# Attention block and octonion feed-forward on one core: score banks shared between heads, masked maxima in two plain operations, two transfers per placed maximum, weight loads on ScalarE's queue, idle products at the start

## The chip, the cores and the metric

The kernel runs on one NeuronCore of one Trainium2 chip. The core has five engines with a queue each: TensorE (PE; its weight loads are listed apart as PEld), VectorE (DVE), ScalarE (ACT), GpSimd (POOL) and SyncE (SP), which here only issues DMA transfers. The metric is the device time of one execution in microseconds. It was measured in five runs, and their median is compared.

## What is computed

The input x is 2 x 1024 x 512, float32. It is normalised per row, and the normalised rows go two ways: through causal attention with 32 heads of 16 and a position bias (ALiBi), and through a feed-forward layer whose weights are octonion-structured and reduced to three values. The result is x + attention x silu(feed-forward).

```
xn = layernorm(x)
qkv = xn @ w_qkv.T + b_qkv ; q, k, v: 32 heads of 16
scores = q k^T / sqrt(16) + slope[h] * (key - 1023), -1e9 above the diagonal
s = softmax(scores) v, then @ w_out.T + b_out
Wq = mean|W| * clip(round(W / mean|W|), -1, 1)      for w_gate, w_up, w_down
M[k, i] = sign(k, i) * Wq[j(k, i)]                  64 blocks from 8
g = silu(M_down (silu(M_gate xn) * (M_up xn)))
out = x + s * g
```

## The kernel before

**Stages.** A lead-in normalises the first batch's eight row blocks (`normal`, lines 205 to 219), transposes them into `xnT` (`norm_item`) and makes the first q, k and v. The attention stage follows, and with it all that can be done beside it: the other q, k and v products (`qk_items`, `v_items`), reducing the weights to signs (`ternary_sum`, `ternary_total`, `ternary_signs`), turning the down weights, normalising the second batch, and the output products. The feed-forward tail (lines 1193 to 1345) comes last and runs gate, up and down over four blocks of 512 rows.

**Units of attention.** A unit is a batch b, a group g of four heads and a half qc of the queries (512 of 1024): 32 units. Each has two passes over its scores. The first pass (`max_items`) finds the row maximum: queries on partitions, a product per tile tl of 128 queries and head i, in a PSUM bank of its own from the two banks of `ps_x`. For qc = 1 the 512 keys to the left are reduced by a plain `tensor_reduce` (line 507). The block up to the diagonal, (tl + 1) x 128 keys wide, goes through one fused operation that adds a mask over the full width, writes the sum to a scratch tile and leaves the maximum in an accumulator, starting from the left maximum (line 510; the profile lists the accumulator's read as an instruction of its own). `split_max` splits the maxima into a high and a low part; `place_max` turns them with four PE transposes, ACT copies them to `mr`, and four DMA transfers issued by POOL, one per head, put them into two extra rows of the unit's q stack (line 551).

The second pass (`exp_step`) has keys on partitions: a product per key tile kt of 128 keys and head (line 571) in a bank of the three of `ps_e`; with the extra rows the product is the score minus its maximum. In the key tiles on the diagonal only the queries from the diagonal on are computed, so widths are 512, 384, 256 and 128, each in its own bank, and a bf16 product of an identity with a triangular mask is added to the first 128 columns (`mask_step`, line 582). ACT takes the exponential of the bank (`exp_of`, line 586) into a tile `p` of four heads. `value_step` multiplies p with v for the four heads in four column strips of PE (line 599) and adds up over the key tiles in one bank; `normalise` divides.

**Order.** The order of PE's queue is written by a planner in the kernel itself (from line 704): it keeps modelled clocks of PE (`now`), ACT and DVE, the times at which banks come free (`e_free`, `x_free`, `m_free`) and a cost for each item, and emits the next item by readiness and priority (`next_max`, `next_exp`, `next_turn`, `next_value`, `next_side`, `next_behind`, `step`). A maximum's placing is taken to have landed 3.5 us after ACT's copy. Matmuls are pinned in program order by `pe`. Instructions that are not pinned may be moved ahead on their engine by the framework's scheduler; in the profile, loads of x and the loads of `bo_sb` and `wo_sb` are issued far ahead of their place in the program.

**Queues.** POOL issues the weight loads (`load_weight`: one transfer and two for a swapped copy), all but the first of the q/k weights (`load_wq`, two transfers each), and the placings. SP issues x, the spills of q and k (`st` to `sp`), the refills of the q and k stacks (`fill_q`, `fill_k`) and the outputs. The weight tiles share the two slots of `vp` with v, so w_u is loaded when the signs of w_g have been stored (`keep_signs`), and w_d when those of w_u have. On POOL, `v_items` fills the v tile with ones (line 379) when its first product is emitted; before that, at line 874, stand the compacting of the second q/k weights (line 131) and the fills of two k stacks.

Of the kernel before, what the change touches and what calls it, by code (L numbers as in the profile page):

```python
# [19 lines left out]
P = 128  # L20
# [39 lines left out]
def kernel(  # L60
# [21 lines left out]

    NP = NG // 2
# [23 lines left out]
    nc.gpsimd.memset(ones, 1.0)  # L107
# [10 lines left out]
    def load_wq(gp, eng):  # L118
        t = wqp.tile([P, 2, KD, 2, 4, 32], F32, tag="wqr", name=f"wqr_{gp[0]}_{gp[1]}")
        for n in range(2):  # L120
            eng.dma_start(
                out=t[:, n].rearrange("p k w h e -> p (k w h e)"), in_=wqk[2 * gp[1] + n]
            )
        wq_raw[gp] = t
# [51 lines left out]
    def load_x(t, eng):  # L176
# [3 lines left out]
        eng.dma_start(out=xt, in_=x[t * P : (t + 1) * P, :])  # L180
# [42 lines left out]
    mask16 = aw.tile([P, P], BF16, name="mask16")  # L223

    def make_mask():
# [5 lines left out]
            pattern=[[1, P]],  # L231
# [5 lines left out]

    def pe(ins):

        return tc.keep_in_program_order(ins)  # L240
# [22 lines left out]
    def load_weight(src, name):  # L263
        w = vp.tile([P, 8, H8], F32, tag="v", name=f"w_{name}")
        nc.gpsimd.dma_start(out=w[0:64].rearrange("p j o -> p (j o)"), in_=src)
        pairs = src.rearrange("p (j s o) -> p j s o", s=2, o=H8)
        swapped = w[64:128].rearrange("p (j s) o -> p j s o", s=2)
        for n in range(2):
            nc.gpsimd.dma_start(out=swapped[:, :, n, :], in_=pairs[:, :, 1 - n, :])
# [100 lines left out]

    def v_items(b, hh):
# [3 lines left out]
        def product(kt, c):  # L375
            if kt == 0 and c == 0:
                v = vp.tile([P, 8, 16 * VC + 16], F32, tag="v", name=f"v_{b}_{hh}")
                v_tiles[b, hh] = v
                nc.gpsimd.memset(v, 1.0)
# [30 lines left out]
    def qk_items(b, gp):  # L410
# [3 lines left out]
        def product(which, c, kt):  # L414
# [20 lines left out]
            if (which, c, kt) == (1, n > 1, KD - 1) and n < B * NP:  # L435
                load_wq((n // NP, n % NP), nc.gpsimd)
# [48 lines left out]
    def max_items(b, g, qc):  # L485
# [3 lines left out]
        def step(tl, i, c):  # L489
            if (tl, i, c) == (0, 0, 0):  # L490
                tiles["mx"] = wk.tile([P, 4, 4], F32, tag="mx", name=f"mx_{b}_{g}_{qc}")
                tiles["part"] = wk.tile([P, 16], F32, tag="part", name=f"mp_{b}_{g}_{qc}")
            t = 4 * qc + tl
            n = 512 if c < qc else (tl + 1) * P
            ps = ps_x.tile([P, 512], F32, tag="x", name=f"s1_{b}_{g}_{t}_{c}_{i}")
            pe(
                nc.tensor.matmul(  # L497
                    ps[:, :n],
                    lhsT=q_of(b, g, qc)[0 : NR - 2, i, tl * P : (tl + 1) * P],
                    rhs=k_of(b, g, c)[0 : NR - 2, i, :n],  # L500
                    start=True,
                    stop=True,
                )
            )
            pm = tiles["part"][:, tl * 4 + i : tl * 4 + i + 1]
            if c < qc:
                nc.vector.tensor_reduce(pm, ps, AX.X, ALU.max)  # L507
                return
            scr = wk.tile([P, 512], F32, tag="scr", name=f"scr_{b}_{g}_{t}_{i}", bufs=1)
            nc.vector.tensor_tensor_reduce(  # L510
                out=scr[:, :n],
                in0=ps[:, :n],
                in1=mask[:, 512 - n : 512],
                scale=1.0,
                scalar=pm if qc else -3.0e38,
                op0=ALU.add,
                op1=ALU.max,
                accum_out=tiles["mx"][:, tl, i : i + 1],
            )

        return [
            (512 if c < qc else (tl + 1) * P, lambda tl=tl, i=i, c=c: step(tl, i, c))
            for tl in range(4)
            for c in range(qc + 1)
            for i in range(4)
        ], tiles

    def split_max(b, g, qc, tiles):

        mx = tiles["mx"]  # L530
        rm = wk.tile([P, 4, 4, 2], F32, tag="rm", name=f"rm_{b}_{g}_{qc}")
        tiles["rm"] = rm
        nc.vector.tensor_copy(rm[:, :, :, 0].bitcast(F32R), mx)
# [884 lines left out]
```

## Time and profile before

| | us |
|---|---|
| median of 5 runs | 1187.65 |
| fastest and slowest run | 1187.31, 1193.19 |
| the profiled execution | 1193.19 |
| its span, first to last instruction | 1191.4 |
| lead-in, until the first score product | 0 to 53.2 |
| attention stage, last exp product of a unit | to 897.1 |
| feed-forward tail, end | 1191.4 |

The mean granted clock of TensorE is 0.972. The costliest groups of the page, with busy time and mean duration, then the idle time of the engine just before them and what ended it:

```profile
L586 ACT ACTIVATE p<-s 128x512 f32<-128x512 f32 (+3 forms) x768 | 324.0, 495 | 294.0 <-PE s L582 189.8
L497 PE MATMUL s<-k_stack,q_stack 126*128 126x512 f32 (+3 forms) x768 | 307.0, 441 | 9.9 <-DVE mx L510 4.9
L571 PE MATMUL s<-q_stack,k_stack 128*128 128x512 f32 (+3 forms) x768 | 253.7, 394 | 31.7 <-DMA q_stack<-mr 21.7
...
L507 DVE TENSOR_REDUCE mp<-s 128x1 f32<-128x512 f32 x256 | 169.1, 686 | 73.8 <-PE s L497 72.4
...
L510 DVE CUSTOM_DVE_ANT_0 scr<-s,mask,mp 128x128 f32<-128x128 f32 (+3 forms) x256 | 140.3, 548 | 82.8 <-PE s L497 67.7
L510 DVE CUSTOM_DVE_ANT_0 scr<-s,mask 128x128 f32<-128x128 f32 (+3 forms) x256 | 125.0, 488 | 100.6 <-PE s L497 82.7
...
L582 PE MATMUL s<-mask,ident 128*128 128x128 bf16 x512 | 68.5, 226 | 0.0
```

A line reads: line of the kernel, engine, operation, result and operands, shapes, count; then busy microseconds and the mean nanoseconds of one; then idle time before. A mean over several shapes ("+3 forms") is no duration of any of them. Durations of matmuls overlap, so the step from one start to the next tells more than the duration.

### The profile page before, as it was taken

The page shows a single profiled execution, that of the slowest core. Times are in us where ns is not written, and L with a number is a line of the kernel's source. Part 1 is how long each engine was busy: PE and PEld are TensorE (multiplying, and loading weights), DVE is VectorE, ACT ScalarE, POOL GpSimd, SP SyncE. Part 2 cuts the span into 40 slices and gives each one's busy share as a digit, 9 for nine tenths or more (in the row PEclk, how much of TensorE's full clock was granted, in tenths as well). Part 3 has the DMA queues.
Part 4 walks back from the last instruction along what each step waited for, and adds up shares of the span by engine and source line. Part 5 has one row for each costly group of instructions (what it writes and reads, how often), then busy time and mean ns, then how long its engine had stood idle before and what let it go on. Part 6 is the DMA issues. An engine that isn't in the chain of part 4 may idle for free.

```text
span 1191.4 us, 16717 instructions
## 1 busy us (share of the span) xinstructions
PE 1089.8 (91%) x5714; PEld 688.5 (58%) x5714; DVE 604.4 (51%) x1714; ACT 526.7 (44%) x1166; POOL 220.9 (19%) x381
## 2 busy tenths in 40 slices
PE   4899589898999799998999999999989999999997
PEld 2544355555645565554555655555445677878775
DVE  5267543666746576565665645667743113131211
ACT  5024475446644346544464444455675213222222
POOL 8311250011110200021100010101100113232322
PEclk9899889999999899999999999999999999999999
DMA  7994445335431743543633515542014112111120
GB/s 251 189 191 147 107 117 108 60 82 99 80 57 48 136 70 56 124 99 75 123 59 53 85 52 122 116 81 50 23 47 152 36 53 73 34 54 54 33 73 35
DMA packets 74964, 104.31 MB, mean 88 GB/s; under 512 B 29040, under 2 KB 32208, under 8 KB 74880
## 3 DMA queue, kind: packets, MB, share of 16 engines
q1 hardware_dynamic: 66336, 87.48, 33.0%
q0 software_dynamic: 8256, 14.72, 5.1%
q8 instruction: 45, 0.74, 0.3%
q10 hardware_dynamic: 288, 1.05, 0.2%
q14 instruction: 39, 0.32, 0.1%
HBM read 69.58 MB, written 33.10 MB: 86 GB/s over the span
## 4 chain that ended last, share of the span: by engine, by line
PE 32%; issue 14%; DMA 2%; ACT 2%; POOL 2%; DVE 2%; DVEq 0%; POOLq 0%; ACTq 0%
PE pg L1253 6%; PE pu L1253 6%; PE pd L1287 5%; PE s L571 4%; PE po L599 3%; PE s L497 3%; PE pout L668 3%; DMA q_stack<-mr 1%; POOL q_stack L551 1%; ACT p L586 1%; DMA out_dram<-y 1%; DVE scr L510 1%; PE s L582 1%; POOL hs L1270 1%; POOL y L1304 0%
## 5 line engine op out<-in xcount | busy, mean ns | idle before, releaser
L586 ACT ACTIVATE p<-s 128x512 f32<-128x512 f32 (+3 forms) x768 | 324.0, 495 | 294.0 <-PE s L582 189.8
L497 PE MATMUL s<-k_stack,q_stack 126*128 126x512 f32 (+3 forms) x768 | 307.0, 441 | 9.9 <-DVE mx L510 4.9
L571 PE MATMUL s<-q_stack,k_stack 128*128 128x512 f32 (+3 forms) x768 | 253.7, 394 | 31.7 <-DMA q_stack<-mr 21.7
L497 PEld LDWEIGHTS s<-k_stack,q_stack 126*128 126x128 f32 x768 | 141.4, 194 | 126.4 <-DVE mx L510 52.4
L507 DVE TENSOR_REDUCE mp<-s 128x1 f32<-128x512 f32 x256 | 169.1, 686 | 73.8 <-PE s L497 72.4
L571 PEld LDWEIGHTS s<-q_stack,k_stack 128*128 128x128 f32 x768 | 143.8, 195 | 98.7 <-ACT p L586 37.5
L510 DVE CUSTOM_DVE_ANT_0 scr<-s,mask,mp 128x128 f32<-128x128 f32 (+3 forms) x256 | 140.3, 548 | 82.8 <-PE s L497 67.7
L510 DVE CUSTOM_DVE_ANT_0 scr<-s,mask 128x128 f32<-128x128 f32 (+3 forms) x256 | 125.0, 488 | 100.6 <-PE s L497 82.7
L551 POOL DMA_DIRECT2D q_stack<-mr x128 | 63.9, 504 | 581.1 <-ACT mr L549 516.9
L599 PE MATMUL po<-p,v 128*32 128x512 f32 (+3 forms) x1536 | 148.9, 497 | 0.0
L426 PE MATMUL pqk<-xnT,wq 128*128 128x512 f32 x256 | 132.2, 616 | 2.5 <-ACT xnT L353 1.4
L1264 DVE SCALAR_TENSOR_TENSOR h<-pu,sc_u,sg 128x512 f32<-128x512 f32 (+1 forms) x44 | 33.1, 751 | 166.4 <-PE pu L1253 160.1
L1270 POOL TENSOR_TENSOR hs<-h,hs 128x512 fp32r<-128x512 f32 (+1 forms) x44 | 57.7, 1311 | 185.5 <-ACT hs L1269 185.5
L599 PEld LDWEIGHTS po<-p,v 128*32 128x32 f32 x1536 | 42.3, 109 | 65.7 <-issue 54.3
L384 PE MATMUL pv<-wv,xnT 128*128 128x256 f32 x256 | 74.4, 409 | 5.5 <-DVE v L395 4.7
L1262 ACT ACTIVATE sg<-pg,sc_g 128x512 f32<-128x512 f32 (+1 forms) x44 | 30.2, 687 | 100.7 <-PE pg L1253 95.7
L582 PE MATMUL s<-mask,ident 128*128 128x128 bf16 x512 | 68.5, 226 | 0.0
L668 PE MATMUL pout<-wo_sb,oT 128*128 128x512 f32 x128 | 62.5, 603 | 0.9 <-ACT oT L659 0.5
L1269 ACT CAST hs<-h 128x512 fp32r<-128x512 f32 (+1 forms) x44 | 27.3, 620 | 75.0 <-DVE h L1264 75.0
L426 PEld LDWEIGHTS pqk<-xnT,wq 128*128 128x128 f32 x256 | 45.1, 194 | 23.9 <-issue 17.1
L441 ACT ACTIVATE st<-pqk,bqk_sb 128x512 fp32r<-128x512 f32 x32 | 22.1, 691 | 78.2 <-PE pqk L426 45.1
L384 PEld LDWEIGHTS pv<-wv,xnT 128*128 128x128 f32 x256 | 48.1, 204 | 14.8 <-DVE v L395 5.1
(157 smaller groups left out, 1130.9 us busy)
## 6 DMA issues: line engine op xcount, KB each, us to landing
sp<-st SPq DMA_DIRECT2D x32, 512.0 KB
q_stack<-sp SPq DMA_DIRECT2D x128, 128.0 KB
k_stack<-sp SPq DMA_DIRECT2D x128, 128.0 KB
wqr<-in_wqk_dram POOLq DMA_DIRECT2D x14, 512.0 KB, 7.2
xt<-in_x_dram SPq DMA_DIRECT2D x16, 256.0 KB
att<-o SPq DMA_DIRECT2D x32, 128.0 KB
ot<-att SPq DMA_DIRECT2D x16, 256.0 KB
proj<-y SPq DMA_DIRECT2D x16, 256.0 KB
```

What stands on the lines that cost most here:

```text
L384: nc.tensor.matmul(ps[:, 0:256], lhsT=xnT[:, c, b * S + kt * P : b * S + (kt + 1) * P], rhs=wv_tiles[2 * b + hh][:, c, :], start=(c == 0), ...
L426: nc.tensor.matmul(ps, lhsT=wq_tiles[b, gp][:, kt, which, :], rhs=xnT[:, kt, b * S + c * 512 : b * S + (c + 1) * 512], start=(kt == 0), st ...
L497: nc.tensor.matmul(ps[:, :n], lhsT=q_of(b, g, qc)[0 : NR - 2, i, tl * P : (tl + 1) * P], rhs=k_of(b, g, c)[0 : NR - 2, i, :n], start=True, ...
L507: nc.vector.tensor_reduce(pm, ps, AX.X, ALU.max)
L510: nc.vector.tensor_tensor_reduce(out=scr[:, :n], in0=ps[:, :n], in1=mask[:, 512 - n : 512], scale=1.0, scalar=pm if qc else -3.0e38, op0=A ...
L551: nc.gpsimd.dma_start(out=q[NR - 2 : NR, i, :].bitcast(F32), in_=mr[2 * i : 2 * i + 2, :].bitcast(F32),)
L571: nc.tensor.matmul(ps[:, :w], lhsT=k[0:NR, i, kt % 4 * P : (kt % 4 + 1) * P], rhs=q[0:NR, i, 512 - w : 512], start=True, stop=(kt < 4 * qc),)
L582: pe(nc.tensor.matmul(ps[:, 0:P], lhsT=ident16, rhs=mask16, start=False, stop=True))
L586: nc.scalar.activation(p_tiles[b, g, qc, kt][:, i, :w], ps[:, :w], AF.Exp, scale=0.25)
L599: nc.tensor.matmul(po[32 * i : 32 * i + 32, 512 - w : 512], lhsT=v[:, kt, h * VC : h * VC + 32], rhs=pr[:, i, :w], start=(kt == 0), stop=( ...
L668: nc.tensor.matmul(ps, lhsT=turned[t][:, c, :], rhs=wo_sb[:, c, :], start=(c == 0), stop=(c == KD - 1),)
L1253: nc.tensor.matmul(ps[:fs, :], lhsT=fw[mt][:, n0 + kt, 0:fs], rhs=part[:, kt, :], start=(kt == 0 and n == 0), stop=(kt == KD - 1 and n == 1),)
```

## The change

It has seven parts.

1. In the first pass the diagonal blocks of several heads share a bank: four heads at 128 keys, two at 256, one at 384 and 512. Their maximum is taken by an addition of the mask in place, on the 128 x 128 diagonal blocks alone, and a plain reduction over the whole bank, one result per head. The left maxima have a tile of their own and are joined in `split_max`.
2. In the second pass the diagonal key tiles are put into cells of full banks: 512; 384 and 128 of the same head; 256 of two heads. One mask product covers both blocks of a bank.
3. The parts of the maxima are laid out by part, and placing takes two transfers of four rows in place of four of two rows.
4. `load_weight` for w_u and w_d and the later `load_wq` are issued by ACT; w_g stays with POOL.
5. The loads of x, of q/k weights, of the three weights, and of `bo_sb` and `wo_sb` are pinned in program order on their queue.
6. `begin_v` fills the v tile with ones; the first is called ahead of the compacting of the second q/k weights.
7. Twenty products of a tile of ones stand first on PE; the ones are set by DVE instead of POOL.

The planner's costs are changed with them: a maximum costs DVE 1.04 per column plus 70, and 135 per head plus 70 for the mask; every exp costs ACT 510; a mask product 55 per block.

```diff
-    nc.gpsimd.memset(ones, 1.0)
+    nc.vector.memset(ones, 1.0)
...
-        eng.dma_start(out=xt, in_=x[t * P : (t + 1) * P, :])
+        pe(eng.dma_start(out=xt, in_=x[t * P : (t + 1) * P, :]))
...
-    mask16 = aw.tile([P, P], BF16, name="mask16")
+    mask16 = aw.tile([P, 2, P], BF16, name="mask16")
...
-    def load_weight(src, name):
+    def load_weight(src, name, eng):
         w = vp.tile([P, 8, H8], F32, tag="v", name=f"w_{name}")
-        nc.gpsimd.dma_start(out=w[0:64].rearrange("p j o -> p (j o)"), in_=src)
+        pe(eng.dma_start(out=w[0:64].rearrange("p j o -> p (j o)"), in_=src))
...
+    def begin_v(b, hh):
+        v_tiles[b, hh] = vp.tile([P, 8, 16 * VC + 16], F32, tag="v", name=f"v_{b}_{hh}")
+        nc.gpsimd.memset(v_tiles[b, hh], 1.0)
...
-                load_wq((n // NP, n % NP), nc.gpsimd)
+                load_wq((n // NP, n % NP), nc.scalar)
...
+        def left(tl, i):
+            if (tl, i) == (0, 0):
+                begin()
+            ps = products(tl, i, 1, 0, 512)
+            nc.vector.tensor_reduce(tiles["left"][:, tl, i : i + 1], ps, AX.X, ALU.max)
+
+        def diagonal(tl, first, count):
+            if (qc, tl, first) == (0, 0, 0):
+                begin()
+            n = (tl + 1) * P
+            ps = products(tl, first, count, qc, n)
+            block = ps[:, :, tl * P : n]
+            nc.vector.tensor_tensor(
+                block,
+                block,
+                mask[:, 384:512].rearrange("p (h n) -> p h n", h=1).to_broadcast([P, count, P]),
+                ALU.add,
+            )
+            nc.vector.tensor_reduce(
+                tiles["mx"][:, tl, first : first + count], ps, AX.X, ALU.max
+            )
...
+            count = (4, 2, 1, 1)[tl]
...
         mx = tiles["mx"]
-        rm = wk.tile([P, 4, 4, 2], F32, tag="rm", name=f"rm_{b}_{g}_{qc}")
+        if qc:
+            nc.vector.tensor_tensor(mx, mx, tiles["left"], ALU.max)
+        rm = wk.tile([P, 4, 2, 4], F32, tag="rm", name=f"rm_{b}_{g}_{qc}")
...
-        for i in range(4):
+        for n in range(2):
             nc.gpsimd.dma_start(
-                out=q[NR - 2 : NR, i, :].bitcast(F32),
-                in_=mr[2 * i : 2 * i + 2, :].bitcast(F32),
+                out=q[NR - 2 + n : NR - 1 + n].bitcast(F32),
+                in_=mr[4 * n : 4 * n + 4, :].bitcast(F32),
             )
...
+    def cells_of(qc):
+        d = 4 * qc
+        return [((kt, 0, 512),) for kt in range(d)] + [
+            ((d, 0, 512),),
+            ((d + 1, 0, 384), (d + 3, 384, 128)),
+            ((d + 2, 0, 256),),
+        ]
...
+        for kt, h, c0, w in pieces:
+            pe(
+                nc.tensor.matmul(
+                    ps[:, c0 : c0 + w],
+                    lhsT=k_of(b, g, kt // 4)[0:NR, h, kt % 4 * P : (kt % 4 + 1) * P],
+                    rhs=q[0:NR, h, 512 - w : 512],
+                    start=(c0 == 0),
+                    stop=(kt < 4 * qc),
+                )
+            )
...
+        if len(pieces) == 1:
+            out, rhs = ps[:, 0:P], mask16[:, 0, :]
+        else:
+            step = pieces[1][2]
+            out = ps.rearrange("p (c n) -> p c n", n=P)[:, 0 :: step // P, :]
+            rhs = mask16
+        pe(nc.tensor.matmul(out, lhsT=ident16, rhs=rhs, start=False, stop=True))
...
+        nc.scalar.activation(p[:, c : c + 512], ps, AF.Exp, scale=0.25)
...
-            lambda: load_weight(w, name),
+            lambda: load_weight(w, name, nc.scalar),
...
+    idle = ps_e.tile([P, 512], F32, tag="e", name="idle")
+    for n in range(20):
+        pe(nc.tensor.matmul(idle[:, 0:P], lhsT=ones, rhs=ones, start=True, stop=True))
...
-    quick(lambda: (compact_wq((0, 1)), add_ring(early, 2, 2)))
+    quick(lambda: (begin_v(0, 0), compact_wq((0, 1)), add_ring(early, 2, 2)))
...
-    later(lambda: nc.gpsimd.dma_start(out=bo_sb, in_=bo.partition_broadcast(P)))
+    later(lambda: pe(nc.gpsimd.dma_start(out=bo_sb, in_=bo.partition_broadcast(P))))
...
-            run_pe("R", ready, max(cost * 0.417 + 18, 108))
-            full = cost == 512 and units[u][2] == 1 and n // 4 % 2 == 0
-            end = run_dve(now[0] + 150, 600 if full else cost * 1.0 + 220)
+            run_pe("R", ready, heads_in * max(cost * 0.417 + 18, 108))
+            end = run_dve(
+                now[0] + 150,
+                heads_in * cost * 1.04 + 70 + (heads_in * 135 + 70) * diagonal,
+            )
```

## The prediction, made before the changed kernel was run

> **What bounds it now.** The page's busy row comes first, then the granted clock by slice, then windows, then the waits of PE, then the timeline where a wait is long.
>
> ```profile
> PE 1089.8 (91%) x5714; PEld 688.5 (58%) x5714; DVE 604.4 (51%) x1714; ACT 526.7 (44%) x1166; POOL 220.9 (19%) x381
> ...
> PEclk9899889999999899999999999999999999999999
> ```
>
> PE is busy nine tenths of the span, and below full clock in early slices. The windows view puts the attention stage, which the change edits, apart from the feed-forward tail, which it leaves alone (286 us):
>
> ```profile
> 45.00:905.00 860.00, 792.18 (x4498) 464.99 (x4498) 519.99 (x1591) 434.57 (x1014) 109.72 (x218) 0.96 0.44 92
> 905.00:1191.00 286.00, 271.99 (x1136) 209.26 (x1136) 64.76 (x75) 74.27 (x119) 78.57 (x59) 0.99 0.16 53
> ```
>
> A busy PE is not a full one. Between 45 and 905 us I took the step from each matmul record's start to the next and subtracted its streaming time: 616 us of 859 is streaming. Some 31 us more are excess at half clock (61 us of half-clock windows); the other 211 us are steps lengthened by waits and by going from one kind of product to another. So the order of PE's queue and the waits in it set the end. PE's matmul waits, then its weight-load waits (which run partly under a matmul, so they bound from above):
>
> ```profile
> PE s L571 <- DMA q_stack<-mr: 21.7, 13, 6.1
> ...
> PE tot_d L281 <- DVE wsum_d L275: 9.5, 1, 9.5
> PE s L571 <- ACT p L586: 9.1, 13, 1.9
> PE s L497 <- DVE mx L510: 4.9, 12, 2.2
> PE pv L384 <- DVE v L395: 4.7, 1, 4.7
> ```
>
> ```profile
> PEld s L497 <- DVE mx L510: 52.4, 168, 2.5
> ...
> PEld s L571 <- ACT p L586: 37.5, 110, 2.3
> ...
> PEld s L497 <- DVE mp L507: 27.1, 82, 1.9
> ```
>
> The reader sees three kinds: a placed maximum that lands late, two long stalls early on, and hundreds of short waits for a score bank.
>
> **The change, part by part.** The sum is made against the profiled execution: 1193.2 us, a span of 1191.4 and 1.8 around it. It is the slowest of five runs, 5.5 above the median of 1187.65; I take the sum off the median.
>
> *Ones filled ahead (begin_v).*
>
> ```profile
> 38.37 1.95 POOL L131 COPY wq<-wqr 128x128 f32<-128x128 f32 x8 [9.90 <-issue]
> ...
> 40.39 3.55 POOL L149 MEMSET k_stack<- 64x2048 f32 x2
> ...
> 44.00 2.02 POOL L379 MEMSET v<- 128x2304 f32 x1
> ...
> 46.53 6.99 PE L384 MATMUL pv<-wv,xnT 128*128 128x256 f32 x18 [4.73 <-DVE v L395]
> ```
>
> POOL idles 9.9 us until PE has read the old wq, then copies, fills two k stacks and only then v. Filled first, v is ready near 31 us and the 4.7 us stall goes. The clock is at half from 45.5 to 52.3 us, behind that stall: 3.4 us more. Next late would be the q rows of the first maxima: their transfer landed at 41.3 us, before the value products end, so nothing new stalls. I take -7, ends -8 and -3.
>
> *Idle products.* Twenty f32 products are 40 records (L281 shows two a product). At 109 to 220 ns (later and first transposes of 128 columns) they last 4.4 to 8.8 us, under PE's wait for the first row block until 12.7. They may warm the clock: the first 16 records of pqk take 8.59 us, the second 16 take 7.13. I take -1; ends -2.3, and +1 if the ones come behind both k fills on DVE.
>
> *Weights on ScalarE's queue.* The down weights before:
>
> ```profile
> 126.14 1.09 POOL L121 DMA_DIRECT2D wqr<-in_wqk_dram  x2 [0.30 <-POOL wq L131]
> ...
> 137.34 0.63 POOL L269 DMA_DIRECT2D w_d<-in_wd_dram  x1 [5.46 <-DMA wqr<-in_wqk_dram]
> ...
> 142.66 0.58 PE L281 MATMUL tot_d<-wsum_d,ones 64*128 64x1 f32 x2 [9.54 <-DVE wsum_d L275]
> ```
>
> The third transfer stood behind wqr's. Without it: the store of w_u's signs landed at 128.5, three issues take 1.8 us, landing 7.4 to 8.6 (w_u's), the sum 1.6: near 140, a stall of 6.6 instead of 9.5, so -3. But the transfer waits for that store, now in ACT's own queue: ACT may stand from 124.2 to 130, with the exps behind it, and PE behind them once three banks are full. Ends -16 (stall and its 13.7 us of half clock gone) and +6. For w_u ACT stands about 73 to 80; its first exp came at 80.6, so 0, worst +3. Seven wq loads put 14 issues of 0.40 us on ACT (5.6 us, under PE where it waits for nothing of ACT), and each may wait for older transfers: the trace has SyncE take 6.15 us for four q fills at 394 us. I take 1 us a load, +7, ends 0 and +45. Pinned x loads come later: blocks 8 and 9 were normalised before the first exp, 10 and 11 together; now up to three more table pairs of 2 x 1.28 us on ACT, +2, ends 0 and +8. The pinned bo and wo loads leave 47 to 67 us; nothing waits for them: 0. Part: +6.
>
> A page speaks against this part. The Trainium skill, "DMA: Bandwidth & Descriptors", section "Issuing engines are not separate DMA queues", says that all transfers share the same engines and another issuing engine saves only sequencer time. The 5.46 us wait above disagrees for this queue; by the page the -3 and the -4 of the next part would be 0.
>
> *Two transfers per placing.*
>
> ```profile
> L551 POOL DMA_DIRECT2D q_stack<-mr x128 | 63.9, 504 | 581.1 <-ACT mr L549 516.9 <-ACT p L586 34.0 <-issue 30.1
> ```
>
> Four issues take 2.0 us, two take 1.0, so the last row lands up to 1 us earlier. Of 13 waits with 21.7 us, 0.6 to 1 us each goes: -8. The longest, 6.1 us at 401.6, stood behind wqr's 1 MB on POOL's queue (landing 7.8 us, 1.4 when quiet): -4. Half-clock windows follow several (216, 298, 342, 400, 544, 643 us: 24 us, 12 lost): -4. Part -16, ends -33 and -6.
>
> *Shared banks.* Score banks fall from 768 + 768 to 608 + 576: a unit's diagonal maxima take 11 banks for 16, its diagonal exps 10 for 16; products and columns stay. The three weight-load waits are 117.0 us over 1536 banks; 23% fewer banks, -27. By the matmul waits of the same rows (17.2 us), -4. Nearer to the first, as steps from score to score are long where no idle is shown: -15.
>
> *DVE's own work.* Steps from start to start when busy: fused add-and-maximum 209, 340, 482, 616 ns for 128 to 512 columns (first half; 276 to 676 in the second), its accumulator read 226. A diagonal costs 10.2 or 11.2 us. After: adds with their durations plus 33 ns, since a reduce reads them (as at a dependent pair of L626 and L627): 724 + 2x454 + 8x318; reduces 7x602 + 4x470; 10.3 us. Level, so 0; it lies beside PE. Over 32 units DVE's ends are -11 us (second halves cost 0.9 less each, first halves nothing) and, with every row's duration counted whole (285, 421, 691 for adds, 686 and 553 for reduces), 10.8 us a diagonal against 9.1 and 10.1, +39; they cost the end only where the cover is gone, which the bank term's far end and the first rival hold.
>
> Here too a page differs: "VectorE: DVE Perf Modes", section "The DRAIN you can't avoid", holds that the next op starts only when the pipe is empty. The trace has reduces of 686 ns start 598 to 607 ns apart, so they overlap. By the page the whole-duration end would hold, and the bank term would be near 0.
>
> *Masks.* 512 records become 320, columns alike. They come in 224 runs of 2.3; at that length 85 runs go. Entering and leaving one costs 57 and 100 ns over streaming: -13. The weight loads' waits there (12.5 us) give -5. I take -9, ends -14 and -3. ACT: four exps of 477, 371, 264, 157 ns make 5.1 us a unit; ten of 477 make 4.8; off the path, 0. The one extra maximum for second halves (0.2 us on DVE, 16 times) has an end of +3: 0.
>
> Sum: -7 -1 +6 -16 -15 -9 = **-42 us**, 1187.65 - 42 = **1146 us**. Ends all at once would be -100 and +50; they aren't one cause.
>
> **Rivals.** *DVE paces the scores.* If maxima set the beat, fewer banks bring nothing: DVE does 10.3 us a diagonal either way, and a PE that waits less for placing waits for DVE. Against it: DVE sits idle 222.8 us for score products. Then -7 -1 +6 -8 -3 = -13: 1175.
>
> *ACT stands behind its own loads.* Nine places (seven wq, w_u, w_d) where transfers wait in the queue that runs the exps. For: SyncE's issues do take up to 6 us for four; the store took 4.3 us to land. Against: PE waits for ACT in 37.5 us of weight loads alone, and qk products stand beside the loads. The other parts give -48; from 5.3 us of PE per place it is lost. At 45 + 6 + 3 + 8 = 62: +14, 1202, slower.
>
> *The order eats it.* Costs in the hand-written order change, so the whole queue is laid anew; new waits may replace old ones: 1187, within 0.3%.
>
> **How the numbers follow.** Chances: forecast 0.59 (its own range 1112 to 1168), DVE 0.20, ACT 0.16, no change 0.05. A measurement tells about 0.3% (3.6 us) from nothing. Faster 0.79, same 0.05, slower 0.16. The range 1110 to 1192 leaves out the slow case and the far fast end.
>
> **What would show it.** Right: v's memset before the copies and no stall at 46 us; 64 placing transfers, their waits under 10 us; 320 masks; the three bank waits below 100 us; an attention stage near 820 us with the tail still 286. Wrong: ACT waiting on transfers for more than 20 us, PE's score waits on ACT grown, tot_d still late, or bank waits above 117 us.

## The result and the profile after

The changed kernel takes 1190.65 us (median of 38 runs, 1184.12 to 1196.33), the kernel before 1187.63 us (64 runs). The ratio is 1.003, interval 1.0019 to 1.0042: slower by about 3.6 us, where 42 less were forecast. Below, every difference is such a ratio to runs of the kernel before on the same chip, times 1187.6 us; the two profiled executions (1193.19 and 1186.91 us) lie on opposite sides of their medians, so their spans are not compared.

The page's busy row and clock row of the changed kernel, then two windows, the attention stage and the tail (columns: window, length, busy time and instructions of PE, PEld, DVE, ACT, POOL, then granted clock, DMA share, GB/s):

```profile
PE 1075.2 (91%) x5562; PEld 684.4 (58%) x5562; DVE 662.5 (56%) x1411; ACT 506.6 (43%) x972; POOL 176.9 (15%) x296
...
PEclk9998988999899999999999998999999999999998
```

```profile
45.00:895.00 850.00, 766.13 (x4292) 450.48 (x4291) 578.50 (x1291) 414.03 (x814) 66.16 (x135) 0.96 0.44 93
895.00:1185.00 290.00, 271.42 (x1139) 208.41 (x1137) 65.20 (x75) 76.62 (x129) 78.61 (x59) 0.98 0.16 55
```

From the first score product to the last value product it is still 843.5 us (845.0 before); it was to be some 25 us less. (The execution before lies 5.6 us above its median and this one 3.7 below, so by the medians the stage is no shorter at all.) PE has less to do there than before (766 us busy for 792), and so has ACT, but VectorE is busy 58 us longer (578.5 for 520.0). The lead-in did get shorter: the first score product starts at 45.8 us instead of 53.2. PE's matmul waits and weight-load waits now (in total, times, longest):

```profile
PE s L501 <- DVE mx L529: 19.9, 47, 1.5
PE pt L673 <- DVE st L446: 18.0, 2, 16.0
PE s L617 <- DMA q_stack<-mr: 7.0, 3, 3.8
...
PE s L617 <- ACT p L639: 5.3, 4, 3.0
...
PE s L501 <- DVE left L515: 2.8, 9, 0.8
...
PE tot_d L283 <- DVE wsum_d L277: 2.0, 1, 2.0
```

```profile
PEld s L617 <- ACT p L639: 28.9, 86, 3.3
...
PEld s L501 <- PE s L617: 20.8, 43, 0.9
PEld s L501 <- DVE left L515: 19.8, 59, 1.4
...
PEld s L501 <- PE s L501: 17.5, 40, 1.0
...
PEld s L501 <- DVE mx L529: 3.2, 8, 0.8
```

Most waits of the table before shrank: placing from 21.7 to 7.0, w_d's sum from 9.5 to 2.0, the exps' from 37.5 to 28.9. Two took their place. PE's score products stand 19.9 us for the maxima of the diagonal, where it was 4.9; and one stall of 16.0 us is new.

The weight loads' wait for those maxima seems to have gone (52.4 before, 3.2 now), but that is a matter of names. The two rows that end in `PE s` are not in the profile before. With a third of 2.5 us they make 40.8 us in 90 waits, and 36.7 of these end within 0.2 us after a reduce of L529, so they are waits for the maxima too. With them the prediction's three bank waits are 88.6 us for 117.0: they fell by 28.4 us, where it had reckoned 27 for 23% fewer banks. PE's own waits on the same three rows, in which no product runs, rose from 17.2 to 28.0. The groups that make the maxima, busy time and mean, then idle time before:

```profile
L515 DVE TENSOR_REDUCE left<-s 128x1 f32<-128x512 f32 x256 | 170.0, 686 | 94.5 <-PE s L501 93.0
L529 DVE TENSOR_REDUCE mx<-s 128x1 f32<-128x384 f32 (+3 forms) x352 | 217.8, 636 | 4.8
...
L523 DVE TENSOR_TENSOR s<-s,mask 128x128 f32<-128x128 f32 (+2 forms) x352 | 120.6, 355 | 96.4 <-PE s L501 92.1
```

217.8 + 120.6 us of plain operations stand where the fused operation took 140.3 + 125.0 and its accumulator reads 42.4.

The new stall, in the timeline (start, duration, instructions, idle before and what ended it; SPq and ACTq are the queues that issue transfers):

```profile
62.58 22.40 SPq L484 DMA_DIRECT2D q_stack<-sp  x4
...
80.69 0.82 ACTq L126 DMA_DIRECT2D wqr<-in_wqk_dram  x2
...
85.50 0.51 SPq L299 DMA_DIRECT2D signs_dram<-w_g  x1
86.75 1.97 SPq L449 DMA_DIRECT2D sp<-st  x2
...
89.24 0.54 ACTq L267 DMA_DIRECT2D w_u<-in_wu_dram  x1
...
93.49 0.69 ACT L445 ACTIVATE st<-pqk,bqk_sb 128x512 fp32r<-128x512 f32 x1 [12.35 <-DMA sp<-st]
95.66 1.56 DVE L277 TENSOR_REDUCE wsum_u<-w_u 64x1 f32<-64x1360 f32 x1 [13.35 <-DMA w_u<-in_wu_dram]
...
97.94 0.90 PE L673 MATMUL pt<-ident,posb 128*128 128x128 f32 x3 [16.04 <-DVE st L446]
```

It is to be read from the top. SyncE needs 22.4 us for four refills of a q stack; the signs of w_g, behind them in its queue, leave at 85.5 us instead of 72.6; w_u can only then be loaded. Behind the signs stand two spills of q and k, so ACT has a free `st` only at 93.5 us. VectorE, which fills the other half of `st`, first stands for w_u, and PE for VectorE. What held SyncE is in the waits of its own queue:

```profile
SPq L471 <- DMA wqr<-in_wqk_dram: 53.9, 4, 30.0
...
SPq L697 <- DMA wqr<-in_wqk_dram: 28.8, 1, 28.8
...
SPq L484 <- DMA wqr<-in_wqk_dram: 20.2, 1, 20.2
```

SyncE's transfers wait 103.8 us in seven places for loads of q/k weights with which they share no data; before, when POOL issued those, it was 1.4 us. Each load now stands in ACT's queue behind the exps, and SyncE's transfers behind the load: the longest wait begins at 561.5 us, and ACT issues the load at 587.8.

### The profile page after: what moved, and what is told of

Same layout as the page of the kernel before. It is cut to its first block, busy times and chain, and to the rows that moved or that the text cites. A ratio compares the mean times of both kernels' runs of the same rounds, so it can differ in the third digit from the quotient of the medians.

```text
span 1185.1 us, 15629 instructions
## 1 busy us (share of the span) xinstructions
PE 1075.2 (91%) x5562; PEld 684.4 (58%) x5562; DVE 662.5 (56%) x1411; ACT 506.6 (43%) x972; POOL 176.9 (15%) x296
## 4 chain that ended last, share of the span: by engine, by line
PE 71%; DVE 11%; DMA 7%; issue 5%; ACT 3%; POOL 2%; SPq 0%; ACTq 0%; DVEq 0%; POOLq 0%
PE s L501 12%; PE s L617 11%; PE po L653 10%; PE pqk L430 8%; PE pg L1322 6%; PE pu L1322 6%; PE pd L1356 5%; PE pout L722 4%; PE pv L388 3%; DVE mx L529 3%; DVE s L523 2%; PE s L634 2%; DMA q_stack<-mr 1%; DVE left L515 1%; PE pm L566 1%
## 5 line engine op out<-in xcount | busy, mean ns | idle before, releaser
L639 ACT ACTIVATE p<-s 128x512 f32<-128x512 f32 x576 | 303.0, 598 | 214.6 <-PE s L634 133.8
L501 PE MATMUL s<-k_stack,q_stack 126*128 126x512 f32 (+3 forms) x768 | 282.5, 431 | 26.5 <-DVE mx L529 19.9
L617 PE MATMUL s<-q_stack,k_stack 128*128 128x512 f32 (+3 forms) x768 | 223.7, 376 | 13.3 <-DMA q_stack<-mr 7.0
L515 DVE TENSOR_REDUCE left<-s 128x1 f32<-128x512 f32 x256 | 170.0, 686 | 94.5 <-PE s L501 93.0
L529 DVE TENSOR_REDUCE mx<-s 128x1 f32<-128x384 f32 (+3 forms) x352 | 217.8, 636 | 4.8
L501 PEld LDWEIGHTS s<-k_stack,q_stack 126*128 126x128 f32 x768 | 135.9, 197 | 123.5 <-issue 34.3
L617 PEld LDWEIGHTS s<-q_stack,k_stack 128*128 128x128 f32 x768 | 137.4, 195 | 70.4 <-ACT p L639 28.9
L523 DVE TENSOR_TENSOR s<-s,mask 128x128 f32<-128x128 f32 (+2 forms) x352 | 120.6, 355 | 96.4 <-PE s L501 92.1
L575 POOL DMA_DIRECT2D q_stack<-mr x64 | 32.0, 505 | 618.0 <-ACT mr L573 586.1
L634 PE MATMUL s<-mask,ident 128*128 128x256 bf16 (+1 forms) x320 | 52.9, 256 | 0.0
```

The source lines that it names most:

```text
L501: nc.tensor.matmul(ps[:, j * n : (j + 1) * n], lhsT=q_of(b, g, qc)[0 : NR - 2, first + j, tl * P : (tl + 1) * P], rhs=k_of(b, g, c)[0 : NR ...
L515: nc.vector.tensor_reduce(tiles["left"][:, tl, i : i + 1], ps, AX.X, ALU.max)
L523: nc.vector.tensor_tensor(block, block, mask[:, 384:512].rearrange("p (h n) -> p h n", h=1).to_broadcast([P, count, P]), ALU.add,)
L529: nc.vector.tensor_reduce(tiles["mx"][:, tl, first : first + count], ps, AX.X, ALU.max)
L617: nc.tensor.matmul(ps[:, c0 : c0 + w], lhsT=k_of(b, g, kt // 4)[0:NR, h, kt % 4 * P : (kt % 4 + 1) * P], rhs=q[0:NR, h, 512 - w : 512], st ...
L634: pe(nc.tensor.matmul(out, lhsT=ident16, rhs=rhs, start=False, stop=True))
```

## The experiments

### Weight loads back on POOL, one kind and both

```diff
e1, e2:  -load_weight(w, name, nc.scalar)               +load_weight(w, name, nc.gpsimd)
e6, e2:  -load_wq((n // NP, n % NP), nc.scalar)         +load_wq((n // NP, n % NP), nc.gpsimd)
```

PE's queue is the same in all of them, instruction by instruction.

> The changed kernel with the loads of w_u and w_d issued by POOL again; the loads of q/k weights stay on ACT. Two theories of the 16.0 us for which PE's transposes of o stand at 97.9 us (and of the 13.7 us of half clock beside them) in the changed kernel. Theory SHARED WAIT: SyncE's refill of a q stack stands 20.2 us for the transfer of wqr, which ACT issues at 80.7 us, behind its exps; the store of w_g's signs behind it on SyncE leaves at 85.5 us, and w_u can't be loaded before. Then w_u is as late from POOL as from ACT: stall of 12 to 17 us still there, SyncE's waits for wqr still near 100 us, time 1186 to 1193. Theory OWN LOADS (the rival of the prediction): ACT stands behind its own load of w_u; then the stall goes, and the time falls by 16 us and 7 us of half clock to about 1168.

> The changed kernel with the seven later loads of q/k weights issued by POOL again; w_u and w_d stay on ACT. SHARED WAIT: SyncE's waits for wqr fall from 103.8 us in 7 to under 5 us, w_g's signs are stored before 76 us, the stall of 16.0 us at 97.9 us goes and with it the half clock: 1190.7 - 16 - 7 = 1168, and to 1160 if the other five waits of SyncE (82.7 us) also made stacks late. OWN LOADS: nothing but noise of the order, 1186 to 1193.

> The changed kernel with all loads of weights issued by POOL again (part 4 of the change undone; the rest stays). SHARED WAIT and OWN LOADS both: the stall at 97.9 us goes, about 1168, or up to 4 us more than the run with only the q/k weights moved back, as placings stand behind 1 MB on POOL's queue again and w_d's third transfer too. A third theory, DVE PACES: VectorE, busy 58 us longer than before, sets the beat of the scores, so that a stall taken away early is waited for later: 1182 or more.

| run | median, us | ratio to before (interval) | the stall, us | SyncE's waits for wqr, us |
|---|---|---|---|---|
| changed kernel | 1190.65 | 1.003 (1.0019 to 1.0042) | 16.0 | 103.8 |
| w_u, w_d on POOL | 1187.68 | 0.9994 (0.9973 to 1.0015) | 13.3 | 105 |
| q/k weights on POOL | 1185.30 | 0.9963 (0.9943 to 0.9983) | 5.0 | 0 |
| all on POOL | 1177.35 | 0.9892 (0.9871 to 0.9914) | 2.2 | 0 |

The run with w_u and w_d on POOL, then the one with the q/k weights there:

```profile
94.24 0.69 ACT L445 ACTIVATE st<-pqk,bqk_sb 128x512 fp32r<-128x512 f32 x1 [12.56 <-DMA sp<-st]
94.96 0.75 DVE L446 SCALAR_TENSOR_TENSOR st<-pqk,bqk_sb,st 128x512 fp32r<-128x512 f32 x1 [12.11 <-ACT st L445]
...
95.77 1.11 PE L673 MATMUL pt<-ident,posb 128*128 128x128 f32 x4 [13.34 <-DVE st L446]
...
96.75 1.56 DVE L277 TENSOR_REDUCE wsum_u<-w_u 64x1 f32<-64x1360 f32 x1 [1.04 <-DMA w_u<-in_wu_dram]
```

```profile
60.30 3.31 SPq L484 DMA_DIRECT2D q_stack<-sp  x4
64.38 0.51 SPq L299 DMA_DIRECT2D signs_dram<-w_g  x1
...
86.25 0.54 ACTq L267 DMA_DIRECT2D w_u<-in_wu_dram  x1
...
92.40 1.12 PE L673 MATMUL pt<-ident,posb 128*128 128x128 f32 x4 [5.03 <-DVE st L446]
```

SHARED WAIT is shown as the cause of SyncE's delay: the same four refills take 3.3 us and the signs leave 21 us earlier. It reaches PE by two ways. In the first run w_u's sum comes only after PE's stall of 13.3 us, which the late spill makes by itself; w_u adds the rest of the 16.0. In the second the spills are in time and w_u alone is late: ACT issues it at 86.25 us, 22 us after the signs, since the load stands in its queue behind exps; POOL in the run with all loads does it at 71.2. Each theory named one cause; taken away alone they give 4.3 and 8.0 us. Part 4 costs (1.003 - 0.9892) x 1187.6 = 16.4 us. What is left of the change without it is worth 12.8 us, so 35 of the forecast 48 are still missing. The runs from here on have all weight loads on POOL, unless they start from the kernel before.

### What VectorE costs

The mask added twice, in the changed kernel:

```diff
             nc.vector.tensor_tensor(block, block, <mask of the diagonal>, ALU.add)
+            nc.vector.tensor_tensor(block, block, <mask of the diagonal>, ALU.add)
```

> The changed kernel with the addition of the mask to the diagonal blocks made twice (the maxima stay the same): 256 more VectorE instructions, some 115 us more of its time, with PE's order untouched. DVE PACES: PE waits for them, at least half comes through: 1245 or more. If VectorE's work lies beside PE with room to spare: under 1200. Between: the slope tells what one us of VectorE costs, and with it what the 58 us that the change added to VectorE cost.

1253.38 us, ratio 1.0533 (1.0509 to 1.0557): 59.7 us more than the changed kernel. VectorE is busy 759.3 us, 96.8 more (352 instructions; the 256 of the expectation was a miscount). So one added us of VectorE costs 0.6 us here. (The second addition also holds each bank longer; the pinned run below tells the two apart.) PE's wait grew where it should, from 19.9 us in 47 to:

```profile
PE s L501 <- DVE mx L535: 63.9, 102, 2.9
```

The fused operation again in the banks of one head (tiles 2 and 3), the shared banks as in the change; first with the planner's old cost for it (f4), then with the costs of the change and so with the same order on PE (g2):

```diff
+            if count == 1:
+                scr = wk.tile([P, 512], F32, tag="scr", bufs=1)
+                nc.vector.tensor_tensor_reduce(
+                    out=scr[:, :n], in0=ps[:, 0, :], in1=mask[:, 512 - n : 512],
+                    scale=1.0, scalar=-3.0e38, op0=ALU.add, op1=ALU.max,
+                    accum_out=tiles["mx"][:, tl, first : first + 1])
+                return
             block = ps[:, :, tl * P : n]
```

> The changed kernel with all weight loads on POOL, and the fused addition and maximum again in the banks of one head (tiles 2 and 3 of a diagonal, 8 of 11 banks), with the planner's old cost for them; the shared banks (tiles 0 and 1) keep the two plain operations. A bank of one head takes VectorE 708 and 842 ns by the steps of the trace before instead of 788 and 920: 0.63 us a unit, 20 us in all. VECTORE COSTS: at 0.65 us each, 13 us less, about 1164. If VectorE lies beside PE: 1174 to 1181.

> The run with the fused operation in the banks of one head, but with the planner's costs of the changed kernel, so that PE's queue is that of the run at 1177.4 us, instruction by instruction. If its 20 us come from VectorE (shorter or undivided operations): 1155 to 1168. If they come from the order that the planner laid anew (the run with 115 ns more cost lost 14 us by its order alone): 1172 to 1180.

f4: 1157.34 us, ratio 0.9744 (0.9723 to 0.9765), 30.4 us less than before: the fastest of all. g2: 1161.21 us, ratio 0.9785 (0.9754 to 0.9816). With PE's queue unchanged the fused operation in 256 banks is worth (0.9892 - 0.9785) x 1187.6 = 12.7 us. By mean steps, from one start to the next where VectorE goes on without a gap, a pair takes 755 ns (384 columns) and 909 ns (512); the fused operation takes 482 and 616 to the read of its accumulator, and 226 more if another fused one comes next, as in 149 of 256 cases. An operation of another kind starts with the read or up to 50 ns after it, if it is ready. That is 15 us less work if every read is counted (128 x (47 + 67) ns), 39 if the other 107 are free; the gain is 0.3 to 0.8 us for each of them. So VECTORE COSTS holds. The attention stage with the pairs, then with the fused operation (same columns as above):

```profile
45.00:885.00 840.00, 769.59 (x4291) 456.27 (x4290) 578.56 (x1291) 413.55 (x808) 77.69 (x154) 0.95 0.45 93
```

```profile
45.00:871.00 826.00, 762.55 (x4295) 454.14 (x4294) 525.91 (x1292) 412.10 (x811) 78.42 (x155) 0.95 0.44 95
```

VectorE's row falls from 578.6 to 525.9 and the stage from 840 to 826, while PE's instructions stay. The 53 us of busy time are more than the steps give, since the durations of a pair overlap with what comes next.

Pairs kept together:

```diff
-            nc.vector.tensor_tensor(block, block, <mask of the diagonal>, ALU.add)
+            pe(nc.vector.tensor_tensor(block, block, <mask of the diagonal>, ALU.add))
```

> The changed kernel with all weight loads on POOL, and the additions of the mask pinned in VectorE's program order, so that a bank's reduce stands right behind its addition; PE's queue is the same, instruction by instruction. In the trace of the changed kernel 211 of 352 pairs have another instruction between them (most often the addition or the reduce of the next bank), and a bank is held for 1.09 us instead of 0.88 (384 columns), 1.30 instead of 1.02 (512), 1.6 instead of 1.16 (two heads). Theory INTERLEAVED PAIRS: this, not VectorE's time, is what the two plain operations cost; 1157 to 1168 here against 1177.4 without the pins. Theory VECTORE'S TIME: its work is the same, so 1174 to 1181.

1192.17 us, ratio 1.0051 (1.003 to 1.0073): 18.9 us slower instead of faster. The theory falls. A bank of 512 columns is held for 1.04 us in the mean instead of 1.22, and yet PE's wait for the maxima rose from 18.9 us in 46 to

```profile
PE s L501 <- DVE mx L529: 31.8, 65, 4.4
```

An addition of 128 columns steps in 324 ns when its own reduce comes next; without the pins half of them (127 of 256) have it next and step in 325 ns, while the step to another operation is 208 ns in the median. The mixing that looked like a fault fills that gap. By mean steps the pinned maxima cost VectorE 493.5 us instead of 480.2. (The pins moved other operations of VectorE a little too, and 13.3 us of work can hardly cost 18.9, so not all of it need be this.)

The planner told the measured cost:

```diff
-                heads_in * cost * 1.04 + 70 + (heads_in * 135 + 70) * diagonal,
+                heads_in * cost * 1.04 + 70 + (heads_in * 135 + 185) * diagonal,
```

> The changed kernel with all weight loads on POOL and 115 ns more per masked bank in the planner's cost of VectorE: steps in the trace are 324 ns from an addition to the reduce behind it and 465 to 598 ns for the reduce, 1326, 1056, 788 and 920 ns for a bank of the four tiles, where the planner counts 1212, 942, 674 and 808. If PE stands for banks that the planner thinks free (19 us of its waits on the maxima of the diagonal), they fall to under 10 us and the time by 5 to 15 us, 1162 to 1172. If the waits only change place: 1174 to 1181, which also tells how much a re-laid order alone moves the time.

1191.42 us, ratio 1.0044 (1.0023 to 1.0065), 18.1 us slower than without: a miss. PE's waits for the maxima of the diagonal did not fall (22.5 us in 40). It shows how far a re-laid order alone moves this kernel, and that differences between kernels of different order are to be read with that in mind.

### Parts undone, and parts alone

f1 puts back the maxima of the kernel before, f2 its second pass. h1, h2, m1 and m2 make one part of the change alone on the kernel before; m3 makes part 2 and the hybrid form of part 1, and none of the others. The edits are those of the diff above, taken part by part.

> The changed kernel with all weight loads on POOL and the maxima of the kernel before (one head in a bank, fused addition and maximum, the planner's old cost for it); what stays is the second pass in full banks, the two transfers, begin_v, the idle products and the pins. It tells what part 1 is worth, beside 1177.4 us of the run that has all but part 4. SHARED BANKS PAY, as the prediction has it (half of its 15 us, and nothing on VectorE): 1182 to 1188 here. VECTORE COSTS (an added us of it cost 0.65 us with the mask added twice; the change keeps it busy 58 us longer): part 1 is a loss, 1150 to 1172 here. Neither: 1174 to 1181.

> The changed kernel with all weight loads on POOL and the second pass of the kernel before (a key tile in a bank, 512 mask products, 768 exps); the maxima in shared banks stay. It tells what part 2 is worth, beside 1177.4 us. By the prediction (9 us of masks and half of the 15 us of banks): 1190 to 1196 here. If the second pass was paced by something else (ACT, the maxima): 1174 to 1182.

> The kernel before with part 2 of the change alone: the second pass in full banks. If gains add up, as the prediction's sum takes it: 12.5 us, as measured when part 2 was undone, so 1174 (the prediction had 16.5). If what a part brings depends on the rest (VectorE's maxima set the beat once the second pass takes less of PE): 1180 or more.

> The kernel before with part 1 of the change alone: diagonal blocks of several heads in a bank, plain addition and reduce. If gains add up: 4.8 us less, 1181. If VectorE's added operations are paid in full and only the full banks of the second pass made room for them: 1186 to 1196.

> The kernel before with part 2 and with part 1 in its hybrid form (fused operation in banks of one head), and none of the other five parts. If these two are where the gain comes from and the other parts (two transfers, begin_v, idle products, pins, without the queue change) bring their 3 us measured alone: 1157 + 3 = 1160, up to 1163. If the other parts cost 10 us, as the sum over parts leaves open: 1145 to 1150.

| run | median, us | ratio to before (interval) | from before, us |
|---|---|---|---|
| all but part 4 (above) | 1177.35 | 0.9892 (0.9871 to 0.9914) | -12.8 |
| the same, old maxima (f1) | 1182.16 | 0.9957 (0.9943 to 0.9971) | -5.1 |
| the same, old second pass (f2) | 1189.90 | 1.0024 (1.001 to 1.0038) | +2.9 |
| second pass alone (m1) | 1184.81 | 0.9967 (0.9945 to 0.9989) | -3.9 |
| shared maxima alone (m2) | 1187.90 | 0.9998 (0.9975 to 1.0022) | -0.2 |
| hybrid maxima and second pass (m3) | 1160.52 | 0.9762 (0.9728 to 0.9795) | -28.3 |

The parts don't add up. Taken out of the whole, the second pass is worth 15.7 us and the maxima 7.7; alone on the kernel before they bring 3.9 and nothing that can be told. It looks as if each paid only where the other is there. But every run of this table has an order of its own, and f3 lost 18.1 us by its order alone, so that is not shown. With the fused operation kept where a bank has one head, the two bring 28.3 us by themselves, almost all of the best run's 30.4.

### Two transfers, ones ahead, pins

> The kernel before with two transfers per placing in place of four, and nothing else; the order stays. The prediction took 16 us for it (0.6 to 1 us from each of 13 waits, 4 of clock, 4 that belong to wqr's place in the queue): 12 without the latter, so about 1175. If the landing and not the issue sets the waits: 1185 to 1189, with PE's waits for the rows still above 18 us.

> The hybrid at 1157.3 us with four transfers per placing again, one for each head with both parts. By the prediction's step an issue of 0.5 us is an issue of waiting: 8 to 16 us more, 1165 to 1173. By the traces of the kernel before with two and with four, a first product that waits comes 5.5 to 5.8 us after ACT's copy with two transfers, as it needs both, and 4.3 to 4.4 with four, while a later head's comes 6.8 to 7.2 after it with four: they cancel, 1154 to 1161.

h1: 1185.64 us, ratio 0.9996 (0.9976 to 1.0016): nothing that can be told. Its wait of PE for the placed rows:

```profile
PE s L571 <- DMA q_stack<-mr: 19.1, 8, 6.8
```

That was 21.7 us in 13. Fewer waits, but longer ones. In the kernel before a stack waits twice: the first head's product comes 4.3 to 4.4 us after ACT's copy (295, 339 us), a later head's 6.8 to 7.2 us after it (298, 342 us). With two transfers the first waiting product comes 5.5 to 5.6 us after it (289, 334 us), as it needs both parts. So the two waits of a stack, 2.8 and 2.5 us together, become one of 2.4 and 2.0. k3, the hybrid with four transfers, takes 1162.49 us, ratio 0.9803 (0.9778 to 0.9827), so on that order two transfers are worth 7 us (the medians differ by 5); neither expectation holds. Its w_d sum is waited for 10.7 us there instead of 6.6, which may be 4 of them.

> The kernel before with the ones of the first v filled ahead of the copies, and nothing else. The prediction took 7 us (4.7 of stall, 2.3 or more of half clock): 1180. If another wait of the lead-in takes its place: 1186 to 1189.

1184.52 us, ratio 0.9977 (0.9955 to 0.9999), 0.1 to 5.3 us less. The first score product is at 46.5 us, 6.6 us earlier, but less than that reaches the end. (In the changed kernel, with the idle products and the pins as well, it is at 45.8.)

```diff
k1, k2:  every pe(...) of part 5 around a load taken off again
```

> The changed kernel with all weight loads on POOL and without the pins of part 5 (loads of x, q/k weights, the three weights, bo and wo float again). PE's products of the second batch's normalised rows stand 6.4 us there against 0.9 in the kernel before, and half clock follows at 180 and 248 us; SyncE waits 41.3 us in its queue for the slots of x. Theory PINS: the sum of the parts measured alone (part 1 -5, part 2 -12.5, begin_v -2, two transfers 0) is -20 where -10 came, and the pins took the other 10: 1163 to 1171 here. Theory ORDER: the difference is the re-laid order: 1174 to 1181.

> The hybrid at 1157.3 us (fused operation in the banks of one head, weights on POOL) without the pins of part 5. PINS: 1145 to 1152. ORDER: 1154 to 1161.

k1: 1184.78 us, ratio 0.9987 (0.997 to 1.0003), with the same order on PE. The wait for the second batch's rows fell from 5.5 to 3.1 us as expected, yet the kernel is 11 us slower than with the pins; its waits for placed rows are 14.2 us in 5 instead of 9.6 in 3. k2: 1156.57 us, ratio 0.9759 (0.9728 to 0.979), no different from the hybrid with pins. The theory PINS falls. Why the pins help the one and not the other is open.

## Why the prediction was wrong, point by point

It forecast 1146 us with 0.79 for faster. A shorter lead-in, 320 masks, 64 placings with less waiting for them, weight-load waits for banks under 100 us and a tail nearly as it was (297 us from the last exp product for 294) all came about, and yet the kernel is no faster. The steps that failed are the cover of VectorE's work, the price of the placings and the price of the weight loads.

- **DVE's own work, 0.** The step priced a diagonal rightly as level ("10.3 us a diagonal after") and then wrote that "it lies beside PE". It doesn't: with the same order on PE, 15 to 39 us less of VectorE's work gave 12.7 us, and 96.8 us more took 59.7. The level price itself was a little high for the kernel before: it counted 226 ns for every read of an accumulator, and after 110 of 512 the next operation starts within 50 ns. The forecast's first rival, "DVE paces the scores", had the mechanism, at 0.20 and 1175 us; the change with the weights back on POOL takes 1177.35. That the numbers are so close is in part luck, since its +6 for the weights and -8 for the placings were not there. The evidence against it, that VectorE sits idle 222.8 us for score products, was misread: e3 and g2 show that VectorE's work costs time although it still idles 185.1 us for them in the changed kernel. The likely reason is that with two banks PE and VectorE wait for each other in turn, so that idle time of both is no room to spare.
- **Shared banks, -15, and masks, -9.** The step leaned on the weight loads' bank waits as the nearer measure, and those fell as counted; PE's own waits, in which no product runs, rose by 10.8 us where 4 less were counted. Undone in the whole the two parts are worth 7.7 and 15.7 us, which is near the forecast's 24 in sum by luck, as the two can't be added: alone they bring 0.2 and 3.9, and together with the fused operation 28.3. Where two passes share PE and each has its own second engine, easing one may move the beat to the other; that reading fits the table, but no run isolates it from the order.
- **Two transfers per placing, -16.** Measured alone: 0.5 us (from 2.9 less to 1.9 more), and 7 on the order of the hybrid. The step counted issues of 0.5 us from the last row. It missed that with one transfer per head a head's product needs only its own, while with one per part every product needs both. The longest wait, put down to wqr on POOL's queue, is still 6.8 us in h1; in the changed kernel it has gone, but also in the run with wqr back on POOL (longest 3.3), so it went with the order and not with the queue.
- **Weights on ScalarE's queue, +6.** It cost 16.4. The sign was right. The shorter wait for w_d's sum came (2.0 us instead of 9.5), but not by the queue: with the loads back on POOL it is 2.6, and in h1, where w_d's third transfer does not stand behind wqr's, it is 8.7. The price was put on the wrong queue: none of the 14 wq transfers took ACT more than 0.5 us to issue, but SyncE waited 103.8 us for them. And w_u, taken as 0 because ACT would stand only briefly, was issued late. The rival "ACT stands behind its own loads" had the direction and not the mechanism: ACT's waits for transfers are 22.7 us, but for SyncE's spill (12.4) and for POOL's stores (10.3). The Trainium skill, "DMA: Bandwidth & Descriptors", section "Issuing engines are not separate DMA queues", says that another issuing engine saves sequencer time only; the forecast weighed it against the 5.46 us wait of w_d. The run with the loads on POOL agrees with the page about the benefit: 2.6 us of waiting for w_d's sum there, 2.0 with them on ACT.
- **Ones filled ahead, -7.** The mechanism was right (first score product 6.6 us earlier, no stall in its place); 2.7 us of it arrive, the near end.
- **Idle products, -1, and pins.** The idle products were not run by themselves. Of a warmer clock nothing is seen: the first 16 records of pqk take 8.71 us with them, for 8.59. The pins, priced at +2 and 0, gain 11 us in one version and nothing that can be told in another.

So of the 46 us between forecast and result, 10 are the weights (16.4 for 6), 16 the placing, 4 the ones (2.7 for 7), and 14 VectorE and the two parts that don't add (24 forecast; the 12.8 of the kernel without part 4, less 2.7 and 0.5 of the others, leave 9.6); the last one is the idle products, whose effect stands in the 9.6, as does that of the pins. This is one way to divide a sum whose parts depend on each other. That the two strongest rivals could both come true at once was not in the sum over cases: each was given with the other absent.

The section "The DRAIN you can't avoid" of "VectorE: DVE Perf Modes" (the Trainium skill), weighed in the prediction, says that the next operation starts when the pipe is empty, but also that one which isn't held back starts earlier. The prediction took the first half alone; with both, its reduces at steps of 598 ns are no contradiction. The pinned run bears on it: an addition steps in 324 ns to its own reduce, and without the pins in 208 to another operation, so independent work in between is worth having.

## What to carry to other kernels

Before an engine's added work is called hidden, look whether it and the bound engine hand the same two or three buffers back and forth: then neither is full, and work added to either may still cost time: here 0.6 us for each us added to VectorE. A quick test is to do the suspected work twice with the same order on the bound engine. When transfers are merged, ask which consumer needs which piece first, and when a load moves to a busy engine's queue, ask who else's transfers may have to wait for it.

The best version here shares banks where several heads fit, keeps the fused addition and maximum where a bank has one head, and leaves the weight loads on POOL: 1157.34 us, 2.6% under the kernel before.

## What the hardware showed beyond that

- SyncE's refills waited up to 30.0 us for the landing of a load that ACT had not yet issued, without shared data. The trace names the wait; by what means the queues are tied is open.
- In the kernel before, the next fused operation never starts sooner than 225 ns after the start of an accumulator's read (336 cases, median 228), but an operation of another kind may start with the read: 110 of the other 176 did within 50 ns.
- Half clock mostly goes with short pauses: in the run with all loads on POOL a pause of PE of 3.0 us that ends at 181.0 us goes with 6.8 us at half clock from 180.1 us on, and two pauses of 1.3 and 1.1 us that end at 289.6 and 292.5 us with 10.2 us from 289.3 us on. But a pause of 2.6 us that ends at 256.5 us has none behind it, so these traces give no length from which it sets in. Half clock takes 90 us of that run's span, 67 of the kernel before, so removing waits elsewhere did not remove it.
